# Routing each token to its two chosen experts: sorted row tiles through DRAM instead of eight dense experts

## The chip, the cores and the metric

The kernel runs on one core of one Trainium2 chip. The metric is the device time of one launch in microseconds (us). TensorE (PE) does the matrix products and writes them to PSUM; VectorE (DVE), ScalarE (ACT) and GpSimd (POOL) are the other compute engines; SyncE (SP) only issues transfers here. Each engine takes its own instructions in the order of the compiled program, and an instruction that waits holds up all that stand behind it on its engine. All data is 32-bit floating point.

## What is computed

One layer works on x of shape (8, 1024, 256): 8 sequences, 1024 time steps, 256 features. Four sublayers follow one another, each on a layer norm of x and added to x: a gated linear attention with its own feed-forward part, a mixture of experts, a small recurrence over time, and the same mixture of experts again.

```python
x = x + attn_a(layernorm(x))      # gated scan over time per head, output projection, GELU FFN
x = x + ffn(layernorm(x))         # mixture of experts "a" in the kernel
x = x + attn_b(layernorm(x))      # h = tanh(x_t B + h A^T), state of 16; y = h C W_out^T + b
x = x + ffn(layernorm(x))         # mixture of experts "b"

def ffn(x):                       # 8 experts, each a 256x256 matrix, 2 per token
    probs = softmax(x @ router_w.T)
    topk_vals, topk_idx = top_k(probs, 2)
    topk_w = topk_vals / (topk_vals.sum(-1) + 1e-6)
    # sum over the two chosen: (x @ W[expert] + its probability) * its weight
```

## The kernel before

The 1024 time steps are cut into 16 groups of 64. A group holds 64 steps of all 8 sequences: 512 tokens, which are 4 tiles (`j`) of 128 tokens by 256 features. The main loop is a software pipeline over 19 steps. Step s does the attention of group s, experts "a" of group s-1, the recurrence of group s-2 and experts "b" of group s-3. The text of the kernel is not the order of execution: the framework's scheduler merges the streams when it compiles, so that each engine has a fixed queue in which the work of four groups is interleaved.

- `layernorm` takes statistics on DVE, one reciprocal square root on POOL (L296, tile `rstd_*`) and the scaling on DVE (L298). So every layer norm passes through POOL's queue.
- `transposed` (L313) turns 128x128 blocks on PE and copies them out on ACT.
- `attention`: projections (L333); the values go through DRAM (`vd`, L475) and come back replicated as four tiles `S` of 1 MB (L481), loaded on SP's queue into four buffers. DVE multiplies (L516), scans over time (16 scans, L524) and multiplies again (L530); PE adds up the state per head (`po`, L535). Then come a norm, the output projection, a second layer norm (`h2`), and the feed-forward part (L578, L342). `others` (called between these pieces) places pieces of the experts' work.
- `moe` routes on the 512 tokens (L379 to L409, some thirty small DVE operations and one ACT exponential). It then multiplies **all** tokens with **all** experts: for each tile `j` four PSUM tiles of two experts each (L418, 512 columns), and DVE adds each expert's part, scaled by a weight that is zero for six of the eight (L427). The bias of a tile is added on POOL (L412).
- `recurrence` is a strict chain of 64 steps per group: a 16x16 matrix product on PE (L613), then a tanh on ACT (L621).

An f32 matrix product is two records in the profile (L418 has 1024 instructions and 2048 records, 1024 in each of its two groups); a transpose is one.

Of the kernel before, what the change touches and what calls it, by code (L numbers as in the profile page):

```python
# [9 lines left out]
F32 = mybir.dt.float32  # L10
AF = mybir.ActivationFunctionType
ALU = mybir.AluOpType
AX = mybir.AxisListType
PSUM = bass.MemoryType.PSUM

P = 128
EPS = 1e-5
# [3 lines left out]
def kernel(  # L21
# [27 lines left out]
    nc = tc.nc  # L49
    NB, T, D = x.shape  # L50
# [6 lines left out]
    NE = router_w.shape[0]  # L57
# [15 lines left out]
    loads = ctx.enter_context(tc.tile_pool(name="loads", bufs=2))  # L73
    ps_mm = ctx.enter_context(tc.tile_pool(name="ps_mm", bufs=2, space=PSUM))
    ps_mx = ctx.enter_context(tc.tile_pool(name="ps_mx", bufs=1, space=PSUM))
    ps_e = ctx.enter_context(tc.tile_pool(name="ps_e", bufs=2, space=PSUM))
# [5 lines left out]
    def mm_tile(name, part="a"):  # L82
        pool = ps_mm if part == "a" else ps_mx
        return pool.tile([P, 512], F32, tag=f"mm_{part}", name=name)

# [21 lines left out]
    rev = const.tile([P, NT, NE], F32, name="rev")  # L107
    for e in range(NE):
        nc.vector.memset(rev[:, :, e : e + 1], float(NE - e))

# [169 lines left out]
    states = ctx.enter_context(tc.tile_pool(name="states", bufs=4))  # L280
    dram = ctx.enter_context(tc.tile_pool(name="dram", bufs=2, space=bass.MemoryType.DRAM))
    small = ctx.enter_context(tc.tile_pool(name="small", bufs=3))
# [68 lines left out]
    def moe(xs, name):  # L351


        yT = transposed(layernorm(xs, name, "m"), name, "m")
        pl = mm_tile(f"pl_{name}", "m")
        for j in range(NT):
            for c in range(KC):
                nc.tensor.matmul(
                    pl[:, j * NE : (j + 1) * NE],
                    yT[:, c, j * P : (j + 1) * P],  # L360
                    rw_t[:, c, :],
                    start=(c == 0),
                    stop=(c == KC - 1),
                )
        logits = pl[:, : NT * NE].rearrange("p (j e) -> p j e", e=NE)

        def row(nm):
            return small.tile([P, NT], F32, tag=f"m_{nm}", name=f"{nm}_{name}")

        def mat(nm):  # L370
            return small.tile([P, NT, NE], F32, tag=f"m_{nm}", name=f"{nm}_{name}")

        def wide(r):
            return r.unsqueeze(2).to_broadcast([P, NT, NE])

        mx, den, m1, m2 = row("mx"), row("den"), row("m1"), row("m2")
        probs, left, sc, one, two = mat("probs"), mat("left"), mat("sc"), mat("one"), mat("two")
        top = row("top")
        nc.vector.tensor_reduce(mx, logits, AX.X, ALU.max)  # L379
        nc.vector.tensor_tensor(probs, logits, wide(mx), ALU.subtract)  # L380
        nc.scalar.activation(probs, probs, AF.Exp)
        nc.vector.tensor_reduce(den, probs, AX.X, ALU.add)
        nc.vector.reciprocal(den, den)
        nc.vector.tensor_tensor(probs, probs, wide(den), ALU.mult)

        nc.vector.tensor_reduce(m1, probs, AX.X, ALU.max)
        nc.vector.tensor_tensor(sc, probs, wide(m1), ALU.is_equal)
        nc.vector.tensor_tensor(sc, sc, rev, ALU.mult)
        nc.vector.tensor_reduce(top, sc, AX.X, ALU.max)
        nc.vector.tensor_tensor(one, sc, wide(top), ALU.is_equal)  # L390
        nc.vector.scalar_tensor_tensor(left, one, -2.0, probs, ALU.mult, ALU.add)
        nc.vector.tensor_reduce(m2, left, AX.X, ALU.max)
        nc.vector.tensor_tensor(sc, left, wide(m2), ALU.is_equal)
        nc.vector.tensor_tensor(sc, sc, rev, ALU.mult)
        nc.vector.tensor_reduce(top, sc, AX.X, ALU.max)
        nc.vector.tensor_tensor(two, sc, wide(top), ALU.is_equal)

        w1r, w2r, rs, bias = row("w1r"), row("w2r"), row("rs"), row("bias")
        nc.vector.tensor_tensor(rs, m1, m2, ALU.add)
        nc.vector.tensor_scalar_add(rs, rs, 1e-6)  # L400
        nc.vector.reciprocal(rs, rs)
        nc.vector.tensor_tensor(w1r, m1, rs, ALU.mult)
        nc.vector.tensor_tensor(w2r, m2, rs, ALU.mult)
        nc.vector.tensor_tensor(one, one, wide(w1r), ALU.mult)
        nc.vector.tensor_tensor(two, two, wide(w2r), ALU.mult)
        nc.vector.tensor_tensor(one, one, two, ALU.add)
        nc.vector.tensor_tensor(w1r, w1r, m1, ALU.mult)
        nc.vector.tensor_tensor(w2r, w2r, m2, ALU.mult)
        nc.vector.tensor_tensor(bias, w1r, w2r, ALU.add)  # L409

        def experts(j):
            nc.gpsimd.tensor_scalar(  # L412
                xs[:, j, :], xs[:, j, :], 1.0, bias[:, j : j + 1], ALU.mult, ALU.add
            )
            for ep in range(NE // 2):
                pe = ps_e.tile([P, 2, D], F32, tag="e", name=f"pe_{name}_{j}_{ep}")
                for c in range(KC):
                    nc.tensor.matmul(  # L418
                        pe,
                        yT[:, c, j * P : (j + 1) * P],  # L420
                        we_t[:, c, 2 * ep : 2 * ep + 2, :],
                        start=(c == 0),
                        stop=(c == KC - 1),
                    )
                for k in range(2):
                    e = 2 * ep + k
                    nc.vector.scalar_tensor_tensor(  # L427
                        xs[:, j, :],
                        pe[:, k, :],
                        one[:, j, e : e + 1],  # L430
                        xs[:, j, :],
                        ALU.mult,
                        ALU.add,
                    )

        return [partial(experts, j) for j in range(NT)]
# [3 lines left out]
    def attention(g, xg, between):  # L440


        between = list(between)

        def others(n):
            for work_of_others in between[:n]:
                work_of_others()
            del between[:n]
# [8 lines left out]
        z = work.tile([P, COLS], F32, tag="z", name=f"z_{g}", bufs=1)  # L457
        nc.scalar.activation(z, pz, AF.Identity, bias=gb2_t)
        az = work.tile([P, COLS], F32, tag="az", name=f"az_{g}", bufs=1)
# [8 lines left out]
        kT = work.tile([P, COLS], F32, tag="kT", name=f"kT_{g}")  # L468
        vT = work.tile([P, KC, COLS], F32, tag="vT", name=f"vT_{g}", bufs=1)
# [76 lines left out]
        oT = work.tile([P, KC, COLS], F32, tag="oT", name=f"oT_{g}", bufs=1)  # L546
        sq = work.tile([P, KC, COLS], F32, tag="sq", name=f"sq_{g}", bufs=1)
# [9 lines left out]
        others(2)  # L557
        for c in range(KC):
            nc.vector.tensor_tensor(oT[:, c, :], po[c], rs, ALU.mult)
        nc.vector.tensor_mul(oT, oT, sgT)  # L560

        xa = work.tile([P, NT, D], F32, tag="xa", name=f"xa_{g}")
# [5 lines left out]
        x1 = work.tile([P, NT, D], F32, tag="x1", name=f"x1_{g}", bufs=4)  # L568
        nc.gpsimd.tensor_add(x1, xg, b2_t.unsqueeze(1).to_broadcast([P, NT, D]))
        nc.gpsimd.tensor_add(x1, x1, xa)  # L570
# [15 lines left out]
        for jp in range(NT // 2):  # L586
            pr = by_token(fT, w2_t, FC, jp, f"pw2_{g}_{jp}")
            js = slice(2 * jp, 2 * jp + 2)
            nc.vector.tensor_add(x1[:, js, :], pr, x1[:, js, :])  # L589
        return x1  # L590
# [32 lines left out]
    def recurrence_out(g, x2):  # L623
        hs = hs_t[g % NHS]
        x3 = work.tile([P, NT, D], F32, tag="x3", name=f"x3_{g}")
        for jp in range(NT // 2):
            py = mm_tile(f"py_{g}_{jp}", "m")
            for jj in range(2):
# [10 lines left out]
                x3[:, js, :], py.rearrange("p (j m) -> p j m", j=2), x2[:, js, :]  # L639
            )  # L640
        return x3
# [3 lines left out]
    x1s, x3s, u_s = {}, {}, {}  # L645
    for step in range(NG + 3):
        ga, gm, gr, gz = step, step - 1, step - 2, step - 3
        between = []
        if 0 <= gr < NG:
            recurrence(gr, u_s.pop(gr))  # L650
        if 0 <= gz < NG:
            x3s[gz] = recurrence_out(gz, x1s.pop(gz))
            between += moe(x3s[gz], f"b{gz}")
        if 0 <= gm < NG:
            between += moe(x1s[gm], f"a{gm}")
        if ga < NG:
            xg = x_next
            if ga + 1 < NG:
                x_next = load_x(ga + 1)
            x1s[ga] = attention(ga, xg, between)  # L660
        else:
            for work_of_others in between:
                work_of_others()
        if 0 <= gz < NG:
            x3 = x3s.pop(gz)
            for b in range(BT):
                nc.sync.dma_start(
                    out=out_v[b, gz * TG : (gz + 1) * TG, :, :],
                    in_=x3[b * TG : (b + 1) * TG, :, :],
                )  # L670
        if 0 <= gm < NG:
            u_s[gm] = recurrence_in(gm, x1s[gm])
# [53 lines left out]
```

## Time and profile before

| what | value |
|---|---|
| median of 3 runs | 2548.77 us (2548.24 to 2550.33) |
| the profiled execution's own time | 2542.61 us |
| its span in the profile | 2540.8 us |
| granted PE clock, mean | 0.88 |
| busy share PE, DVE, ACT, POOL | 86%, 63%, 25%, 12% |
| indirect transfers | none |
| transfers issued by POOL | 2, both at the start |

A line of the profile's groups names the source line, engine, operation, and the tiles (output, then inputs), the shapes, the count, the busy time in all, and the mean of one. What stands behind the second bar is the time that the engine idled just before these instructions, and what ended that idle time. A line of the timeline gives the start, the duration, and the same names. The busy time of PE is no measure of its peak, since matrix products overlap with one another; the distance from one start to the next in a dense row of them is.

### The profile page before, as it was taken

Reading aid. Unit: us, or ns where it says so; the run is one execution under the profiler, and the core shown is the slowest. Engines: PE = TensorE matmul, PEld = TensorE weight load, DVE = VectorE, ACT = ScalarE, POOL = GpSimd, SP = SyncE. Lnnn points to the kernel's source line nnn. Section 1 sums busy time; section 2 is a strip of 40 time slices with the busy share of each in tenths; the row PEclk is TensorE's granted clock in tenths of the full one; section 3 lists DMA queues with packets and bytes.
Section 4 is the critical chain, followed back from the end, with each engine's and each line's share of the span. In section 5 each row is a group of like instructions: output and inputs, shape, how many; then the busy total and the mean of one; then the engine's idle time right before and its main releaser. Section 6 shows DMA issues by size and latency. Waiting matters only on the chain.

```text
span 2540.8 us, 22420 instructions
## 1 busy us (share of the span) xinstructions
PE 2183.9 (86%) x7505; PEld 966.4 (38%) x7505; DVE 1600.2 (63%) x3877; ACT 631.4 (25%) x1657; POOL 305.7 (12%) x264
## 2 busy tenths in 40 slices
PE   3478898988989898898989889898998989988987
PEld 1234342433434243343434334243343434334333
DVE  4675858567574857757475674856747576573534
ACT  2123242141413213131321313214131221312010
POOL 1101010121111111101111201112011111110000
PEclk9598988989999898988979798897988979798978
DMA  5130303030302103030020302103030030300000
GB/s 155 26 75 9 75 9 75 17 75 17 75 9 50 35 16 75 17 75 9 26 58 17 75 9 61 27 13 75 17 75 9 1 75 9 75 9 1 9 0 17
DMA packets 37893, 98.39 MB, mean 39 GB/s; under 512 B 4666, under 2 KB 25203, under 8 KB 29587
## 3 DMA queue, kind: packets, MB, share of 16 engines
q1 hardware_dynamic: 33664, 94.64, 15.7%
q10 hardware_dynamic: 4034, 2.17, 0.3%
q8 instruction: 61, 1.00, 0.2%
q14 instruction: 54, 0.43, 0.1%
q0 software_dynamic: 80, 0.14, 0.0%
HBM read 80.17 MB, written 16.78 MB: 38 GB/s over the span
## 4 chain that ended last, share of the span: by engine, by line
PE 62%; DVE 21%; ACT 7%; issue 5%; POOL 2%; DMA 2%; ACTq 0%; POOLq 0%; SPq 0%; DVEq 0%
PE pe_b L418 18%; PE pe_a L418 9%; DVE x L427 6%; PE pu L613 5%; DVE S L524 5%; PE pw L342 4%; PE po L535 3%; ACT hs L621 3%; PE pf L578 3%; PE pu L597 2%; PE pg L333 2%; PE py L630 2%; PE pz L333 2%; PE pt_h L313 2%; DVE S L516 2%
## 5 line engine op out<-in xcount | busy, mean ns | idle before, releaser
L418 PE MATMUL pe_b<-we,yT_b 128*128 128x512 f32 x1024 | 570.2, 674 | 32.8 <-DVE x L427 27.7
L418 PE MATMUL pe_a<-we,yT_a 128*128 128x512 f32 x1024 | 466.7, 604 | 23.6 <-DVE x L427 14.2
L427 DVE SCALAR_TENSOR_TENSOR x<-pe_b,one_b,x 128x256 f32<-128x256 f32 x512 | 240.5, 476 | 225.3 <-PE pe_b L418 220.8
L613 PEld LDWEIGHTS pu<-hs,at 16*16 16x16 f32 x2046 | 115.5, 94 | 599.3 <-ACT hs L621 348.8
L613 PE MATMUL pu<-hs,at 16*16 16x8 f32 x2046 | 216.9, 176 | 140.0 <-ACT hs L621 139.7
L621 ACT ACTIVATE hs<-pu 16x8 f32<-16x8 f32 x1024 | 176.0, 172 | 637.6 <-PE pu L613 634.2
L524 DVE TENSOR_TENSOR_SCAN S<-decay,S 128x512 f32<-128x512 f32 x256 | 306.2, 1210 | 0.0
L427 DVE SCALAR_TENSOR_TENSOR x<-pe_a,one_a,x 128x256 f32<-128x256 f32 x512 | 244.4, 478 | 97.5 <-PE pe_a L418 87.6
L418 PEld LDWEIGHTS pe_a<-we,yT_a 128*128 128x128 f32 x1024 | 191.1, 192 | 265.2 <-issue 232.2
L418 PEld LDWEIGHTS pe_b<-we,yT_b 128*128 128x128 f32 x1024 | 185.9, 205 | 251.2 <-issue 194.7
L516 DVE TENSOR_TENSOR S<-S,kT 128x2048 f32<-128x2048 f32 x64 | 145.6, 2275 | 16.4 <-DMA S<-vd 16.4
L535 PE MATMUL po<-S,head_pad 128*32 128x512 f32 x512 | 122.1, 828 | 39.2 <-DVE S L530 38.6
L530 DVE TENSOR_TENSOR S<-S,qT 128x2048 f32<-128x2048 f32 x64 | 146.1, 2283 | 0.0
L412 POOL TENSOR_SCALAR x<-x,bias_a 128x256 f32<-128x256 f32 x64 | 102.0, 1608 | 295.4 <-DVE bias_a L409 295.4
L570 POOL TENSOR_TENSOR x<-x,xa 128x1024 f32<-128x1024 f32 x16 | 37.6, 2347 | 815.5 <-DVE mv_h L292 803.8
L321 ACT ACTIVATE yT_h<-pt_h,lnb,lnw 128x512 f32<-128x512 f32 x64 | 47.9, 776 | 323.6 <-PE pt_h L313 323.5
L578 PE MATMUL pf<-yT_h,w 128*128 128x512 f32 x256 | 121.4, 621 | 1.7 <-ACT yT_h L321 1.7
L589 DVE TENSOR_TENSOR x<-pw,x 128x512 f32<-128x512 f32 x32 | 22.1, 691 | 147.1 <-PE pw L342 147.1
L549 ACT ACTIVATE sq<-po 128x512 f32<-128x512 f32 x32 | 19.1, 597 | 380.8 <-PE po L535 380.8
L342 PE MATMUL pw<-w,fT 128*128 128x256 f32 x512 | 113.1, 379 | 0.0
L342 PEld LDWEIGHTS pw<-w,fT 128*128 128x128 f32 x512 | 97.3, 190 | 20.1 <-issue 7.7
L638 DVE TENSOR_TENSOR x<-py,x 128x512 f32<-128x512 f32 x32 | 22.1, 690 | 123.2 <-PE py L630 123.2
(193 smaller groups left out, 2318.1 us busy)
## 6 DMA issues: line engine op xcount, KB each, us to landing
S<-vd SPq DMA_DIRECT2D x64, 1024.0 KB, 12.8
x<-in_L_attn_a_x_dram SPq DMA_DIRECT2D x32, 256.0 KB, 3.9
vd<-vT SPq DMA_DIRECT2D x16, 512.0 KB, 2.8
out_dram<-x SPq DMA_DIRECT2D x32, 256.0 KB, 3.2
we<-_ffn_expert_weights_dram SPq DMA_DIRECT2D x8, 256.0 KB, 4.7
w<-in_L_attn_a_W_dram ACTq DMA_DIRECT2D x2, 512.0 KB, 6.3
wo<-in_L_attn_a_Wo_dram SPq DMA_DIRECT2D x16, 16.0 KB, 2.3
wv_raw<-in_L_attn_a_Wv_dram ACTq DMA_DIRECT2D x1, 256.0 KB, 3.8
```

What stands on the lines that cost most here:

```text
L333: nc.tensor.matmul(ps, w[:, c, :], rhsT[:, c, :], start=(c == 0), stop=(c == KC - 1))
L342: nc.tensor.matmul(ps[:, jj * D : (jj + 1) * D], lhsT[:, c, j * P : (j + 1) * P], w[:, c, :], start=(c == 0), stop=(c == n_k - 1),)
L412: nc.gpsimd.tensor_scalar(xs[:, j, :], xs[:, j, :], 1.0, bias[:, j : j + 1], ALU.mult, ALU.add)
L418: nc.tensor.matmul(pe, yT[:, c, j * P : (j + 1) * P], we_t[:, c, 2 * ep : 2 * ep + 2, :], start=(c == 0), stop=(c == KC - 1),)
L427: nc.vector.scalar_tensor_tensor(xs[:, j, :], pe[:, k, :], one[:, j, e : e + 1], xs[:, j, :], ALU.mult, ALU.add,)
L516: nc.vector.tensor_tensor(S_f, S_f, kT.unsqueeze(1).to_broadcast([P, VQ, COLS]), ALU.mult)
L524: nc.vector.tensor_tensor_scan(S_f[:, j, :], decay_f, S_f[:, j, :], 0.0, ALU.mult, ALU.add)
L530: nc.vector.tensor_tensor(S_f, S_f, qT.unsqueeze(1).to_broadcast([P, VQ, COLS]), ALU.mult)
L535: nc.tensor.matmul(po[c][32 * j : 32 * j + 32, :], head_pad[:, NH * (1 - i) : NH * (1 - i) + 32], S_f[:, j, :], start=(i == 0), stop=(i == 1),
L578: nc.tensor.matmul(pf, w1_t[:, c, f * P : (f + 1) * P], h2T[:, c, :], start=(c == 0), stop=(c == KC - 1),)
L613: nc.tensor.matmul(pu[:, t, :], at_t, before, start=False, stop=True, skip_group_check=True,)
L621: nc.scalar.activation(hs[:N, :, t], pu[:, t, :], AF.Tanh)
```

## The change

The experts' part is computed for the two chosen experts only.

- Each token is copied twice into a DRAM buffer, at places that are sorted by expert. Routing computes the places: counts per tile by two small matrix products (`pn`, new lines 467 and 468), running sums, and each expert's rows rounded up to whole tiles of 128. A register list `eidi` says which expert owns each row tile.
- The copy is an indirect DMA on POOL's queue: two for each tile of 128 tokens (new L535), 128 rows of 1 KB each.
- A piece `expert(ip)` loads two row tiles from DRAM on SP's queue (L548), reads the two expert numbers into PE registers (L549), transposes (L560), copies on ACT (L564), multiplies by the register-chosen expert (L568, 256 columns), copies on ACT (L576) and stores to a second DRAM buffer (L577).
- `combine` fetches each token's two results with two indirect DMAs per tile (L584, tile `got`, two buffers) and adds them, scaled, on DVE (L590).
- A call now spans a block of two groups; nine blocks of 1, 2, 2, 2, 2, 2, 2, 2 and 1 groups take 12 steps in place of 19. A block of two groups has 2048 chosen rows and 24 row tiles (12 pieces); a block of one has 1024 rows and 16 row tiles (8 pieces).
- The tile bias moves from POOL to ACT (L542). To make room in SBUF, x is updated in place and has nine buffers, the `S` tiles have three buffers, and some tiles share space. The keys and queries are projected ahead of the values.

```diff
+BLOCKS = [1] + [2] * 7 + [1]
...
-    states = ctx.enter_context(tc.tile_pool(name="states", bufs=4))
+    states = ctx.enter_context(tc.tile_pool(name="states", bufs=3))
+    rows = ctx.enter_context(tc.tile_pool(name="rows", bufs=2))
...
-        def experts(j):
-            nc.gpsimd.tensor_scalar(
-                xs[:, j, :], xs[:, j, :], 1.0, bias[:, j : j + 1], ALU.mult, ALU.add
-            )
-            for ep in range(NE // 2):
-                pe = ps_e.tile([P, 2, D], F32, tag="e", name=f"pe_{name}_{j}_{ep}")
+        rows_in, rows_out = (t[: NTL * P, :] for t in rows_dram[name[0]])
+        for j in range(NJ):
+            for s in range(2):
+                nc.gpsimd.indirect_dma_start(
+                    out=rows_in,
+                    out_offset=bass.IndirectOffsetOnAxis(ap=posi[:, s, j : j + 1], axis=0),
+                    in_=ys[j // NT][:, j % NT, :],
+                    in_offset=None,
+                )
+            x_j = xs[j // NT][:, j % NT, :]
+            nc.scalar.activation(x_j, x_j, AF.Identity, bias=bias[:, j : j + 1])
...
+        def expert(ip):
+            r = rows.tile([P, 2, D], F32, tag="r", name=f"r_{name}_{ip}")
+            nc.sync.dma_start(out=r, in_=in_v[:, 2 * ip : 2 * ip + 2, :])
+            _, ids = nc.values_load_multi_w_load_instructions(
+                eidi[0:1, 2 * ip : 2 * ip + 2],
+                engines=[mybir.EngineType.PE],
...
+            for k in range(2):
                 for c in range(KC):
                     nc.tensor.matmul(
-                        pe,
-                        yT[:, c, j * P : (j + 1) * P],
-                        we_t[:, c, 2 * ep : 2 * ep + 2, :],
+                        pe[:, k, :],
+                        rT[:, k, c, :],
+                        we_t[:, c, bass.ds(ids[k], 1), :],
                         start=(c == 0),
                         stop=(c == KC - 1),
                     )
...
+            nc.sync.dma_start(out=out_v_[:, 2 * ip : 2 * ip + 2, :], in_=ro)
+
+        def combine():
+            for j in range(NJ):
+                x_j = xs[j // NT][:, j % NT, :]
+                for s, w in enumerate((w1r, w2r)):
+                    e = rows.tile([P, D], F32, tag="got", name=f"got_{name}_{j}_{s}")
+                    nc.gpsimd.indirect_dma_start(
+                        out=e,
+                        out_offset=None,
+                        in_=rows_out,
+                        in_offset=bass.IndirectOffsetOnAxis(ap=posi[:, s, j : j + 1], axis=0),
+                    )
                     nc.vector.scalar_tensor_tensor(
-                        xs[:, j, :],
...
+                        x_j, e, w[:, j : j + 1], x_j, ALU.mult, ALU.add
                     )
...
+    for step in range(NK + 3):
+        ba, bm, br, bz = block(step), block(step - 1), block(step - 2), block(step - 3)
...
+        for i, g in enumerate(ba):
+            n = -(-len(between) // (len(ba) - i))
+            mine, between = between[:n], between[n:]
...
+            attention(g, xg, mine)
+            x1s[g] = xg
+        for work_of_others in between + last:
+            work_of_others()
```

## The prediction

> **What bounds the kernel now.** I read the page's engine shares first, then the chain that ended last.
>
> ```profile
> span 2540.8 us, 22420 instructions
> ...
> PE 2183.9 (86%) x7505; PEld 966.4 (38%) x7505; DVE 1600.2 (63%) x3877; ACT 631.4 (25%) x1657; POOL 305.7 (12%) x264
> ...
> PE 62%; DVE 21%; ACT 7%; issue 5%; POOL 2%; DMA 2%; ACTq 0%; POOLq 0%; SPq 0%; DVEq 0%
> ```
>
> PE holds 62% of the chain, DMA 2%, POOL 2%: PE sets the pace, and no transfer is on the path. The groups by line show the experts, and POOL's bias op beside each kind of DVE work:
>
> ```profile
> L418 PE MATMUL pe_b<-we,yT_b 128*128 128x512 f32 x1024 | 570.2, 674 | 32.8 <-DVE x L427 27.7 <-DVE S_last L527 2.5 <-DVE one_a L390 0.7
> L418 PE MATMUL pe_a<-we,yT_a 128*128 128x512 f32 x1024 | 466.7, 604 | 23.6 <-DVE x L427 14.2 <-DVE S_last L527 5.6 <-issue 3.5
> L427 DVE SCALAR_TENSOR_TENSOR x<-pe_a,one_a,x 128x256 f32<-128x256 f32 x512 | 244.4, 478 | 97.5 <-PE pe_a L418 87.6 <-POOL x L412 2.4
> L412 POOL TENSOR_SCALAR x<-x,bias_a 128x256 f32<-128x256 f32 x64 | 102.0, 1608 | 295.4 <-DVE bias_a L409 295.4
> L412 POOL TENSOR_SCALAR x<-x,bias_b 128x256 f32<-128x256 f32 x64 | 29.6, 479 | 250.9 <-DVE bias_b L409 250.9
> ```
>
> The mean of one overlaps its neighbours, so I price PE from dense rows of the timeline (start, duration, count last):
>
> ```profile
> 2287.67 9.61 PE L418 MATMUL pe_a<-we,yT_a 128*128 128x512 f32 x22
> 2305.43 7.07 PE L342 MATMUL pw<-w,fT 128*128 128x256 f32 x32
> 2312.34 0.60 PE L313 MATMUL pt_yr<-ident,y_yr 128*128 128x128 f32 x4
> ```
>
> One 512-column record takes 9.61/22 = 0.437 us, a 256-column one 0.221, a transpose 0.15.
>
> **The compute that goes and comes.** Out: 2048 records x 0.437 = 895 us of PE; 1024 DVE additions, 485 us (244.4 + 240.5); 132 us of POOL (L412). In: 18 calls have 2x(2x8 + 7x12) = 200 pieces. Each piece is 4 transposes (0.60) and 8 records of 256 columns (1.77): 2.37 us, 474 us in all. Rounding to whole tiles is in that: 24 row tiles stand against 64 dense ones, not 16. Each piece also makes PE read registers, 200 reads, which the trace does not show. Bounds: 0, and 1.28 us (an ACT table load, the trace's one row of an engine fetching before it goes on). I take the middle, 0.64: 128 us. The skill's page "DMA: Bandwidth & Descriptors" (Latency and other measured facts) gives such a load a floor of some 600 ns; by it the term would be 120. PE is left with 895 - 474 - 128 = 293 us less. DVE gains 256 additions x 0.48 = 123 and loses 485; routing adds some 22 small operations of 0.2 us per call, but 18 calls replace 32, about nothing. ACT gains 400 copies x 0.58 (L317's mean) and 128 bias operations at 0.4 (below the 0.58 of a copy twice as wide), 283 us: 36% busy, in cover.
>
> Small edits, at nothing: SP issues 400 transfers more (two take 1.30 us: 260 us), under waits for POOL. With three `S` buffers the fourth load waits until the first tile is used up; it is needed some 28 us after the first, and a load takes 12.8 (issue rows): without that cover, up to 12.8 per group. Keys and queries ahead of the values put `vd` off by 8 records, 3.5 us per group, where an attention is exposed.
>
> If PE still set the end: 2541 - 293 = 2248.
>
> **The 512 indirect transfers.** They are what the trace of before cannot show. The compiled order settles their form. All 512 stand in POOL's one queue. Each of a block's 16 scatters waits for the semaphore of the scatter before it, as all write one DRAM tensor. The gathers go two at a time, since `got` has two buffers, each freed by its addition on DVE. And POOL's queue also holds the `rstd` of every layer norm: what stands behind a waiting scatter is the attention's next norm, then DVE and PE behind that. The nearest rows are issues (KB each, us to landing last) and POOL's own time to issue one:
>
> ```profile
> 1.28 0.74 POOL L131 DMA_DIRECT2D b<-in_L_attn_a_b_dram  x1 [0.35 <-issue]
> ```
> ```profile
> x<-in_L_attn_a_x_dram SPq DMA_DIRECT2D x32, 256.0 KB, 3.9
> vd<-vT SPq DMA_DIRECT2D x16, 512.0 KB, 2.8
> out_dram<-x SPq DMA_DIRECT2D x32, 256.0 KB, 3.2
> b<-in_L_attn_a_b_dram POOLq DMA_DIRECT2D x1, 128.0 KB, 5.3
> ```
>
> - A scatter: 2.8 at least (`vd`, issue included), 0.74 + 5.3 = 6.04 at most (POOL's own transfer, in the crowded start). I take the store out of mid-run plus POOL's issue, 0.74 + 3.2 = 3.94: same direction, same stage.
> - A gather, half of a round of issue, landing and addition: (0.74 + 2.8 + 0.48)/2 = 2.01 to (0.74 + 5.3 + 0.48)/2 = 3.26; I take (0.74 + 3.9 + 0.48)/2 = 2.56.
>
> Scatter and gather together, s = 6.50, between 4.8 and 9.3. There are 256 of each.
>
> The rows are of larger transfers (256 KB for 128), which speaks for less. L412 speaks for more: beside the attention's scans the same POOL operation takes 1608 ns for 479. Some 60% of the 88 scatters of experts "b" in steps 3 to 8 lie beside scans (37.6 of 63 us); were the issue stretched as L412 is, 0.74 to 2.5, that is 53 x 1.76 = 93 us. I let the two cancel and keep the 93 for the upper end. The skill's page "SBUF — State Buffer" (A bandwidth-pool intuition that's wrong (but worth ruling out)) speaks against the change too: GpSimd is locked out of writing its descriptors while DVE holds the shared port, 620 ns becoming 3100. No transfer here shows it; by that figure 53 scatters would cost 131 us more.
>
> **Where they stand on the path.** In a full step the compiled order of POOL and DVE is a ring: layer norms and routing of "b"; 16 scatters of b; the second norm of the step's first attention; 16 scatters of a; 16 gathers of b; the second norm of the second attention; 16 gathers of a; then the next step's norms. b's pieces run under a's scatters (63 us against 12 x 4.5 = 54), a's under b's gathers and the second attention; the recurrence (128 x 0.47, a dense step of L613 and L621, is 60 us) under b's scatters. So a full step is 16 pairs twice, 32 s, plus what POOL waits for:
>
> ```profile
> 952.30 1.02 POOL L296 TENSOR_TENSOR rstd_b<-ve_b,neghalf 128x4 f32<-128x4 f32 x1 [0.17 <-DVE mv_a L292]
> ...
> 969.96 1.85 POOL L412 TENSOR_SCALAR x<-x,bias_b 128x256 f32<-128x256 f32 x4 [13.99 <-DVE bias_b L409]
> ```
> ```profile
> 29.67 1.02 POOL L296 TENSOR_TENSOR rstd_h<-ve_h,neghalf 128x4 f32<-128x4 f32 x1 [3.06 <-DVE ve_h L294]
> ...
> 112.82 1.02 POOL L296 TENSOR_TENSOR rstd_h<-ve_h,neghalf 128x4 f32<-128x4 f32 x1
> ```
>
> From a norm to routed takes 17.7 us for one group; with two groups and more operations I take 27. The norms between take about 8 after b's scatters and 15 before a's gathers (908.66 to 922.67 in the timeline). Together 50. Where DVE's order puts the second attention's scans behind the gathers of b, their 38 us (16 x 1.21 + 8 x 2.28) and the 18 to the next norm are exposed: 56 in steps 3 and 5, 30 in step 4 (scans partly earlier), none in 6 and 7. The sum, from step 3 on:
>
> - Steps 0 to 2: one attention alone takes 83 us (the two rows above). Its second norm at 113, feed-forward 20 and routing 27 make 160; then 8 scatters, 32 of pieces, 8 gathers, the scans behind them 56, feed-forward and routing 55, 16 scatters, the next attention's projections and scans 72, 16 gathers and routing 27: 402 + 24 s.
> - Steps 3 to 7: 24 s + 106, 32 s + 80, 32 s + 106, 32 s + 50, 32 s + 50; step 8: 32 s + 50; step 9: 24 s + 35.
> - Steps 10 and 11, with nothing to run b's pieces under: 16 s + 75 and 8 s + 55.
>
> That is 1009 + 256 s. With s = 6.50: 1009 + 1664 = 2673 us of span. The profiled execution lies 1.8 above its span, the median 6.2 above that, so 2673 + 8 = 2681; I say 2680.
>
> So the end moves from PE to POOL's queue: PE's 293 us come off, and are not on the path any more. A full step takes 258 to 314 us, against 304 for two groups before (`rstd_b` goes from 345.0 to 2323.66 in 13 steps, 152 each). The loss stands at the end, where the pipeline empties in steps of two groups: steps 8 to 11 sum to 735; before, the same stretch, from the fifteenth group's attention on, took some 2541 - (345 + 12 x 152) = 372.
>
> **Rivals.**
> - *Short transfers, faster.* Quiet 128 KB transfers come in near the `vd` row. The ring equals the time of before at s = (2541 - 1009)/256 = 5.98, and decides for faster below it. At s = 4.8 it gives 2238, where PE (2248) takes over: about 2256 with the 8. For it: the rows I took are of twice the bytes. Against: an indirect transfer must also read its indices, which no row prices.
> - *Long transfers, far slower.* Descriptors held up by DVE or made row by row: s above 8 gives over 3065, at 9.3 with the 93 above 3491. For it: the 1608 against 479.
> - *The recurrence sets the pace.* Two groups in one step are 128 links. At 0.47 us they are 60 us; with one 512-column product between (1.19, from 2458.59 to 2459.78 in the timeline) 152. Both lie inside a step of 258, so it changes nothing; the time stays 2680.
>
> **How the numbers follow.** The forecast, s from 5.98 to 8, gives 2553 to 3065 and has 0.45; short transfers 0.36; long ones 0.16; that the two effects meet within 0.2% (5 us, about what a measurement can tell from no change) 0.03. Slower is 0.45 + 0.16 = 0.61. The range goes down to the PE bound, 2250, and up to 3250, s = 8.7, which leaves out about a tenth at each end.
>
> **What would show it.** Right: POOL's queue waiting for its own transfers (`rows_a_in`, `rows_b_in`, `got`) on top of the chain, PE below 65% busy, first scatters to last some 63 us per 16, a step of two groups at 258 to 314 us, some 735 us from step 8 on. Wrong: PE still over 80% busy with L568 and L560 on the chain; consecutive scatters under 3 us apart, or over 6; or PE waiting long at the register read L549.

## The result: 363 us slower, and the profile after

| | before | after |
|---|---|---|
| median of the runs | 2549.55 us (4 runs) | 2912.27 us (4 runs) |
| ratio after to before, 95% interval | | 1.141 [1.137, 1.145] |
| span of the profiled execution | 2540.8 us | 2909.4 us |
| mean granted TensorE clock | 0.881 | 0.749 |

The forecast was 2680 us, in a range of 2250 to 3250. The sign was right and the time lies inside the range, but 363 us were lost where 131 were expected. First the page's engine shares and its costliest groups for the kernel after (columns as before):

```profile
span 2909.4 us, 25546 instructions
...
PE 1925.9 (66%) x8057; PEld 1113.3 (38%) x8057; DVE 1306.0 (45%) x3081; ACT 887.6 (31%) x2182; POOL 739.2 (25%) x649
...
L568 PE MATMUL pe_a<-we,rT_a 128*128 x800 | 233.7, 438 | 55.7 <-ACT rT_a L564 54.8
L535 POOL DMA_INDIRECT rows_a_in<-y_a,posi_a x128 | 150.4, 1175 | 440.1 <-DMA rows_a_in<-y_a,posi_a 274.5
L535 POOL DMA_INDIRECT rows_b_in<-y_b,posi_b x128 | 149.7, 1169 | 432.2 <-DMA rows_b_in<-y_b,posi_b 217.9
L568 PE MATMUL pe_b<-we,rT_b 128*128 x800 | 218.6, 418 | 44.5 <-ACT rT_b L564 43.0
L584 POOL DMA_INDIRECT got_b<-rows_b_out,posi_b x128 | 132.5, 1035 | 312.0 <-DVE x L590 144.0
L584 POOL DMA_INDIRECT got_a<-rows_a_out,posi_a x128 | 126.1, 985 | 251.3 <-DVE x L590 104.2
```

PE is down from 86% to 66% of the span, as the forecast wanted. The scatters (L535) and gathers (L584) are on POOL, with 1436 us of idle time before them. Only 492 of those are scatters waiting for the scatter before (274.5 + 217.9). The other large waits are for routing (363 us for `posi_a` and `posi_b`), for the additions on DVE that free `got` (248) and for expert outputs (183). (The chain of waits breaks off on this page after the last few instructions, all at 0%, so I read POOL's queue in its place.) The timeline of POOL in step 6, the first that the prediction took at 32 s + 50; the last bracket is the idle time before the row and what ended it:

```profile
1572.06 0.94 POOL L584 DMA_INDIRECT got_a<-rows_a_out,posi_a  x1 [0.77 <-DVE x L590]
...
1631.39 2.94 POOL L535 DMA_INDIRECT rows_b_in<-y_b,posi_b  x1 [39.40 <-DVE posi_b L507]
1636.06 1.60 POOL L535 DMA_INDIRECT rows_b_in<-y_b,posi_b  x1 [1.72 <-DMA rows_b_in<-y_b,posi_b]
...
1642.68 0.96 POOL L535 DMA_INDIRECT rows_b_in<-y_b,posi_b  x1 [1.70 <-DMA rows_b_in<-y_b,posi_b]
1645.34 0.96 POOL L535 DMA_INDIRECT rows_b_in<-y_b,posi_b  x1 [1.71 <-DMA rows_b_in<-y_b,posi_b]
...
1711.86 0.96 POOL L535 DMA_INDIRECT rows_a_in<-y_a,posi_a  x1 [20.57 <-DVE posi_a L507]
```

One scatter takes 0.96 us to issue and 1.70 until it has landed: 2.66 from one to the next (1642.68 to 1645.34). At the start of the series, where DVE's scans and products on `S` run at the same time, the issue is stretched to 1.6 to 2.9 us. The two large brackets are waits for routing, of b and of a. With the same reading of the whole step, from the last gather of one step to the last of the next:

| POOL in that step, 1573 to 1886 us | measured | forecast |
|---|---|---|
| norms and routing of b | 58 | 27 |
| 16 scatters of b, with one norm among them | 60 | 63 |
| routing of a | 21 | 0 |
| 16 scatters of a | 63 | 63 |
| gathers of b (with 5 of waiting for stores) and of a | 50 + 31 | 41 + 41 |
| norms between them | 29 | 8 + 15 |
| sum | 313 | 258 |

Why routing takes 58 and not 27 is in DVE's timeline, and why a's starts so late too:

```profile
1597.85 0.22 DVE L452 TENSOR_TENSOR sc_b<-sc_b,rev 128x64 f32<-128x64 f32 x1
1597.99 1.22 DVE L689 TENSOR_TENSOR_SCAN S<-decay,S 128x512 f32<-128x512 f32 x1
1599.13 0.19 DVE L453 TENSOR_REDUCE top_b<-sc_b 128x8 f32<-128x64 f32 x1
1599.24 1.21 DVE L689 TENSOR_TENSOR_SCAN S<-decay,S 128x512 f32<-128x512 f32 x1
...
1692.84 1.38 DVE L345 TENSOR_SCALAR y_a<-x,mv_a,rstd_a 128x256 f32<-128x256 f32 x4 [6.78 <-DMA rows_b_in<-y_b,posi_b]
...
1711.41 0.17 DVE L507 CAST posi_a<-pos_a 128x16 uint32<-128x16 f32 x1
```

Between two routing operations of 0.2 us the compiled order puts a scan of 1.2. And a's normed rows (`y_a`) wait for b's last scatter: the tag `y_m` has two buffers, both hold b's rows until they are scattered.

Step by step (ends read at the last gather of a, in POOL's timeline): steps 0 to 2 end at 591 us (forecast 558), steps 3 to 7 take 318, 324, 340, 313 and 307 (forecast 262, 288, 314, 258, 258), step 8 takes 285 (258), steps 9 to 11 431 (477). At the end of step 7 the kernel is 24 us behind the kernel before at the same attention (2193 against 345 + 12 x 152 = 2169), and what follows takes 716 us against 372. Those are not the same work: with blocks of two, experts "b" have then been done for 9 groups, where the kernel before has done them for 12. `dense2` below tells the two apart.

### The profile page after: what moved, and what is told of

It is laid out like the page before. It is cut to its first block, busy times and chain, and to the rows that moved or that the text cites. A ratio compares the mean times of both kernels' runs of the same rounds, so it can differ in the third digit from the quotient of the medians.

```text
span 2909.4 us, 25546 instructions
## 1 busy us (share of the span) xinstructions
PE 1925.9 (66%) x8057; PEld 1113.3 (38%) x8057; DVE 1306.0 (45%) x3081; ACT 887.6 (31%) x2182; POOL 739.2 (25%) x649
## 5 line engine op out<-in xcount | busy, mean ns | idle before, releaser
L568 PE MATMUL pe_a<-we,rT_a 128*128 x800 | 233.7, 438 | 55.7 <-ACT rT_a L564 54.8
L535 POOL DMA_INDIRECT rows_a_in<-y_a,posi_a x128 | 150.4, 1175 | 440.1 <-DMA rows_a_in<-y_a,posi_a 274.5
L535 POOL DMA_INDIRECT rows_b_in<-y_b,posi_b x128 | 149.7, 1169 | 432.2 <-DMA rows_b_in<-y_b,posi_b 217.9
L568 PE MATMUL pe_b<-we,rT_b 128*128 x800 | 218.6, 418 | 44.5 <-ACT rT_b L564 43.0
L568 PEld LDWEIGHTS pe_a<-we,rT_a 128*128 128x128 f32 x800 | 164.0, 216 | 127.6 <-ACT rT_a L564 84.2
L584 POOL DMA_INDIRECT got_b<-rows_b_out,posi_b x128 | 132.5, 1035 | 312.0 <-DVE x L590 144.0
L681 DVE TENSOR_TENSOR S<-S,kT 128x2048 f32<-128x2048 f32 x64 | 145.9, 2279 | 122.1 <-DMA S<-vd 106.9
L568 PEld LDWEIGHTS pe_b<-we,rT_b 128*128 128x128 f32 x800 | 154.3, 204 | 106.9 <-ACT rT_b L564 83.1
L584 POOL DMA_INDIRECT got_a<-rows_a_out,posi_a x128 | 126.1, 985 | 251.3 <-DVE x L590 104.2
L560 PE MATMUL prt_a<-ident,r_a 128*128 128x128 f32 x400 | 70.5, 304 | 165.7 <-DMA r_a<-rows_a_in 165.7
L590 DVE SCALAR_TENSOR_TENSOR x<-got_b,w1r_b,x 128x256 f32<-128x256 f32 x64 | 35.1, 548 | 295.1 <-DMA got_b<-rows_b_out,posi_b 295.0
L576 ACT COPY ro_a<-pe_a 128x512 f32<-128x512 f32 x100 | 58.5, 585 | 297.3 <-PE pe_a L568 208.2
L560 PE MATMUL prt_b<-ident,r_b 128*128 128x128 f32 x400 | 65.8, 290 | 100.3 <-DMA r_b<-rows_b_in 100.3
L560 PEld LDWEIGHTS prt_a<-ident,r_a 128*128 128x128 f32 x400 | 54.8, 157 | 195.0 <-issue 157.5
```

The source lines that it names most:

```text
L535: nc.gpsimd.indirect_dma_start(out=rows_in, out_offset=bass.IndirectOffsetOnAxis(ap=posi[:, s, j : j + 1], axis=0), in_=ys[j // NT][:, j % ...
L560: nc.tensor.transpose(pt[:, n * P : (n + 1) * P], r[:, k, c * P : (c + 1) * P], ident)
L568: nc.tensor.matmul(pe[:, k, :], rT[:, k, c, :], we_t[:, c, bass.ds(ids[k], 1), :], start=(c == 0), stop=(c == KC - 1),)
L576: nc.scalar.copy(ro, pe)
L584: nc.gpsimd.indirect_dma_start(out=e, out_offset=None, in_=rows_out, in_offset=bass.IndirectOffsetOnAxis(ap=posi[:, s, j : j + 1], axis=0),)
L681: nc.vector.tensor_tensor(S_f, S_f, kT.unsqueeze(1).to_broadcast([P, VQ, COLS]), ALU.mult)
```

## The experiments

All are single runs of one kernel unless an interval is given; the kernel before took 2547 to 2571 us beside them. The four runs of the changed kernel lie between 2904 and 2917, so differences of some 13 us say nothing. Gains are counted from 2912.

**What the transfers cost.** Three kernels leave them out; in `no_gather` the addition reads `ys[j // NT][:, j % NT, :]`.

```
-            for s in range(2):
-                nc.gpsimd.indirect_dma_start(out=rows_in, ...)        # no_scatter, no_indirect
-                    e = rows.tile([P, D], F32, tag="got", ...)
-                    nc.gpsimd.indirect_dma_start(out=e, ...)
+                    e = ys[j // NT][:, j % NT, :]                      # no_gather, no_indirect
```

`no_scatter`: 

> The 256 scatters are left out (the sorted rows stay zero); routing, loads, products, gathers and additions stay. In the changed kernel's profile the scatters hold POOL for 792 us (150 + 150 busy, 274 + 218 waiting for their own transfer). Theory A, the transfers in POOL's queue lie on the path: the 425 us of the a scatters come off at least, so 2250 to 2500 us. Theory B, the path runs through the waits between the engines (norms, routing and two attentions a step in a fixed order), and transfers fill time that would be spent waiting anyway: under 200 us come off, over 2700.

Measured 2622.79.

`no_gather`: 

> The 256 gathers are left out; the additions that combine read the normed rows in SBUF in their place. The gathers hold POOL for 639 us (133 + 126 busy, the rest waiting for the additions, without the 183 that wait for expert outputs). Theory A: 400 to 640 us come off, 2270 to 2500. Theory B: the waits for expert outputs and for the second attention stay, over 2700.

Measured 2683.61.

`no_indirect`: 

> Scatters and gathers both left out; all products, loads and stores of rows stay, and the additions read the normed rows. Theory A: nothing but PE is left to set the pace, 2300 to 2400 us, PE over 80% busy. Theory B: 2600 us or more, PE under 75% busy and POOL waiting for DVE's norms as before.

Measured 2372.56. So the scatters are worth 290 us, the gathers 229, both together 540, little more than the sum of 519. But these are 540 of the 1051 us (792 for scatters alone, 259 for the gathers' issue) that they hold POOL at the least. For either alone neither theory had it (A forecast 410 to 660 off for the scatters, B under 200); with both out A's 2300 to 2400 holds, with PE at 79% for its "over 80%". These kernels also cut what hung on the transfers: without scatters nothing holds the two buffers of `y` for them, and without gathers the additions no longer wait for expert outputs. So the 540 us are the transfers together with their couplings, not the transfers alone.

`open_scatter` keeps all work and takes the wait away, as the rows of a block differ:

```
+                tc.declare_no_dep(sc_i.ins, group=f"sc_{name}", reason=...)
+                tc.add_to_no_dep_group(f"sc_{name}", sc_i.ins)
```

> All work kept; the scatters of one block, which write different rows, no longer wait for one another (each waits only for the one eight before it). A scatter should hold POOL for its issue, about 1.0 + 0.3 us, in place of 3.1. Theory A: 256 x 1.8 = 460 us less on POOL, of which the half that lies beside the first attention's scans may stay hidden: 2450 to 2690 us. Theory B: 2800 to 2900.

Measured 2802.24, a gain of 110. The timeline of POOL in its step from 1493 to 1815 us:

```profile
1558.57 2.94 POOL L535 DMA_INDIRECT rows_b_in<-y_b,posi_b  x1 [46.75 <-DVE posi_b L507]
...
1566.24 0.96 POOL L535 DMA_INDIRECT rows_b_in<-y_b,posi_b  x1 [0.30 <-issue]
1567.51 0.96 POOL L535 DMA_INDIRECT rows_b_in<-y_b,posi_b  x1 [0.30 <-issue]
...
1613.59 0.96 POOL L535 DMA_INDIRECT rows_a_in<-y_a,posi_a  x1 [28.70 <-DVE posi_a L507]
...
1670.99 1.03 POOL L588 DMA_INDIRECT got_b<-rows_b_out,posi_b  x1 [27.73 <-DMA rows_b_out<-ro_b]
```

The edit did what it should: 1.27 us from scatter to scatter (1566.24 to 1567.51), 16 in 26 us for b and 20 for a, where they took 60 and 63. And the step still takes 322 us: the 77 us came back as longer waits for b's routing (46.8 us, 39.4 in step 6 above), for a's (28.7 for 20.6), for the expert outputs (27.7 for 5.4) and, behind the lines shown, for a norm of the second attention (59.2 for 15.3). Theory A falls here as a law for the step; theory B's 2800 to 2900 holds, at its lower edge.

**What else could it be: the blocks, the recurrence.** `dense2` keeps the blocks of two and the new attention and computes all eight experts (the old `experts` loop over a block's tiles, no rows in DRAM).

> Blocks of two groups and the changed kernel's attention, but all eight experts computed for every token as before: no scatter, no gather, no register reads. If the blocks cost only the longer emptying at the end, some 150 us, and the keys and queries that are projected twice 56 us of PE: 2700 to 2760. If the blocks cost nothing: 2550 to 2610. If most of the 363 us lost comes from the blocks: over 2800.

Measured 2579.79, in the range for blocks that cost nothing: 30 us, with the doubled projections in it. Where they lie shows in the copy that ends each quarter of an attention's scans (before, `dense2`, after; the number before the semicolon is the start of the last one):

```profile
L527 DVE COPY S_last<-S x64: 170/183/380, 65.0 to 2252.5; 128x32 f32<-128x32 f32 x64
L581 DVE COPY S_last<-S x64: 166/186/287, 64.1 to 2120.8; 128x32 f32<-128x32 f32 x64
L692 DVE COPY S_last<-S x64: 163/186/195, 78.5 to 2269.4; 128x32 f32<-128x32 f32 x64
```

From there to the end of the span it is 288 us before, 457 in `dense2` and 640 after. So 169 of the 352 us by which the emptying is longer come with the blocks of two, which leave more work over; `dense2` had gained 132 us ahead of this point for it. Against `dense2` the sparse kernel loses 149 us up to the last scans and 183 behind them. `blocks1` is the reverse, `BLOCKS = [1] * 16`:

> The changed kernel with blocks of one group (16 blocks; 8 pieces per call in place of 12 per two groups, 256 pieces of 2.37 us in place of 200). Theory A: the same 512 transfers, a shorter emptying at the end: 2750 to 2900. Theory B: the waits of a step (norms, routing, expert outputs) come once per group instead of once per two: 3000 or more.

Measured 3086.66: the steps' waits come per step, as theory B had it (the 28% more pieces are in it too).

`no_recur` replaces the linked loop by one `tanh` per group, and `before_no_recur` does the same to the kernel before:

> The recurrence's chain is left out: one tanh per group in place of 64 linked pairs of a product and a tanh. Theory of the prediction: the links lie beside other work, 2880 to 2912. Rival: the 1024 links, 0.47 us each when nothing stands between (481 us in all), hold PE's and ACT's queues, in order, ahead of routing and experts: 2500 to 2750.

Measured 2734.57, 178 less. That looked like a cause.

> A control for no_recur: the kernel before, with the recurrence's chain left out in the same way. If the 178 us that no_recur gained on the changed kernel are a cost of the new order, this gains clearly less, under 100 us (2450 or more). If the links cost both kernels the same, it gains 150 to 220 us, as PE was busy with them for 217 us: 2330 to 2400; then they are no part of what the change lost.

Measured 2337.58, 209 less. The links cost the kernel before even more: they are no part of the loss.

**Order and buffers, one at a time.** Each is the changed kernel with one edit.

```
scans_after: +  with tc.issue_after(<the cast to posi of b and of a>): <the first attention's scans>
a_first:     the call and the additions of a are written ahead of those of b
adds_after:  +  with tc.issue_after(<last scan product of the step>): <combine of b and of a>
four_y:      y_m bufs=4 in place of 2; kT, qT bufs=1 in place of 2
```

`scans_after`: 

> The first attention's scans are queued on DVE behind the routing of both calls of the step (order alone; no work is changed). In the changed kernel's steps of two groups POOL waits 39 to 49 us for posi_b and 17 to 22 for posi_a, because scans of 1.2 and 2.3 us stand between routing operations of 0.2. Theory B (waits between engines set the pace): 20 to 30 us less in each of the five full steps and some in the others, 2750 to 2820 us. Theory A (the transfers set the pace; a wait saved before them returns behind them, as the scans then run later): within 30 us of 2912.

Measured 2883.13, 29 less: just inside A's range. Theory A's reason, that the scans then run later and what waits for them does too, was not traced further.

`a_first`: 

> In each step the call for a is put ahead of the call for b, and its additions too (order alone). What b computes goes to the output only; what a computes is what the recurrence and the next step's b need. Theory B (the order in the queues makes the waits): a's scatters no longer wait 60 us behind b's, 2750 to 2850 us. Theory A (the transfers set the pace, whatever their order): within 30 us of 2912.

Measured 2800.02, 112 less, with not a transfer changed: theory B.

`adds_after`: 

> The additions of gathered rows are queued on DVE behind the scans of the step's last attention (order alone). In the changed kernel DVE waits 407 us for gathered rows of b, and POOL 53 to 84 us a step in steps 3 and 5 for the second attention's norm behind them. Theory B: 80 to 150 us less, 2760 to 2830. Theory A: within 30 us of 2912.

Measured 2860.51, 52 less: between the two ranges.

`four_y`: 

> The normed rows y have four buffers in place of two (keys and queries one each, to make room); nothing else. With two, the call for a can't write its normed rows before b's scatters have read theirs, so a's routing starts behind b's last scatter: POOL waits 17 to 22 us for posi_a in each full step, 59 in step 3, 154 in all. If that coupling is on the path: 2760 to 2850 us. If it only moves the wait elsewhere: 2880 to 2912.

Measured 2797.98, 114 less. With `a_first`'s 112 it is the largest of the four; the two can't be told apart, and both bear on a's wait behind b. In its timeline b's and a's scatters alternate in one series, and the wait for `posi_a` falls from 20.6 to 3.4 us.

**All transfers cheaper, then in another order.** `open_deep` is `open_scatter` with `got` at `bufs=6` and the second projection of keys and queries kept alone; `all_orders` adds `a_first` and `adds_after`.

`open_deep`: 

> All work kept: scatters of a block not waiting for one another, six buffers for gathered rows in place of two, keys and queries projected once. Each transfer should hold POOL for some 1.3 us in place of 3.1 and 2.5, 700 us less over 512. Theory A: 2400 to 2600 us. Theory B: what POOL saves comes back as waits for norms, routing and expert outputs, as it did with open scatters alone (2802): 2720 to 2800.

Measured 2777.46: theory B. The deep gathers and the spared projections are worth 25 us on top of the open scatters.

`all_orders`: 

> open_deep with a ahead of b and the additions behind the last attention's scans. If both the transfers' time and the order of the queues make the loss, each hides behind the other and only both together free the step: 2400 to 2550 us. If the recurrence's links in PE's queue hold the rest: 2600 or more.

Measured 2739.84, in the range of "2600 or more", but the links need not be why. In its waits two faults of this order show: a's additions had been pinned behind the scans with b's (POOL waited 337.5 us in `got_a` for them), and `posi_b` came 54 to 57 us after a's scatters, since `y` still had two buffers.

`uncoupled` mends both: `four_y`, `scans_after`, `a_first` and `open_deep` together, only b's additions behind the last scans, and one buffer for the attention's own normed rows.

> All work kept: open scatters, six buffers for gathered rows, keys and queries once, four buffers for y (one for the attention's), a ahead of b, both routings ahead of the first attention's scans, b's additions behind the last attention's scans. If the couplings through buffers and queue order are what puts 540 us of transfers on the path, a full step falls to the 267 to 280 us that it has without indirect transfers, against 302 to 313: 2450 to 2580 us. If a step stays at 300 or more, something not yet named holds it: 2700 or more.

Measured 2544.28: all 512 transfers are there, and the kernel is 368 us faster than the changed one, as much as the change had cost. `open_deep` (2777) has the same open scatters, gather buffers and projections, so the order and the buffers of `y`, keys and queries alone are worth 233 us here. They were not run together with the slower transfers, so how much of the 233 needs the cheap ones is open. The windows of two of its full steps and of its emptying (start and end, length, then busy time and instructions of PE, PEld, DVE, ACT, POOL, granted clock, DMA share, GB/s):

```profile
1153.50:1439.90 286.40, 233.24 (x978) 131.03 (x977) 160.04 (x366) 104.49 (x267) 97.04 (x81) 0.82 0.40 114
1439.90:1726.90 287.00, 233.32 (x978) 131.43 (x976) 160.11 (x366) 104.42 (x267) 95.34 (x80) 0.82 0.40 114
2007.10:2542.60 535.50, 359.95 (x1774) 225.53 (x1773) 156.66 (x484) 156.86 (x510) 178.52 (x171) 0.75 0.39 118
```

A full step takes 287 us with all transfers, and PE is busy for 233 of them. Without indirect transfers (`no_indirect`) it took 267 to 280. So nearly all of the transfers' time can hide in a full step. What remains is the emptying, 535 us with PE two thirds busy; behind the last scans it is 472 us, against 457 in `dense2`.

**The emptying.** `uncoupled_tail` ends in three blocks of one, `BLOCKS = [1] + [2] * 6 + [1] * 3`:

> The same with the last two blocks of two and one replaced by three blocks of one group, so that the pipeline empties in steps of one group. From the last attention on, all_orders took some 545 us against 372 before the change. If the emptying is a chain of one block's transfers and products per step, it shrinks: 40 to 100 us less than uncoupled. If the waits of a step cost the same for one group as for two (as blocks1 showed, 3087): the same or slower.

Measured 2547.09: the same. The emptying did shrink, from 472 to 357 us behind the last scans, but these came 118 us later (2188 for 2070). `short_tail` is `uncoupled` with the order changed after the last attention (products behind the links; b's gathers and additions behind the next block's scatters and routing):

> uncoupled, with the emptying put in order: after the last attention a block's products stand on PE behind the recurrence's links, and b's gathers and additions behind the next block's routing and scatters (a second tensor for expert outputs of b). In uncoupled the last 535 us go to a chain in which b's three blocks follow one another and the links, 0.47 us when dense, take over a us each between products (128 in 170 us). If that chain sets the end: 60 to 130 us less, 2410 to 2485. If transfers and loads of one block after another set it: 2530 to 2545.

Measured 2556.97 (10 runs), ratio to the kernel before 0.999 [0.995, 1.003]: the same, so this order does not shorten the emptying. It put the products so far back that b's next norm waited 48 us for them; whether a better order exists was not tried, and the links are not ruled out by it.

`dense_tail` is `uncoupled` with the last four calls dense, `dense=not ba`, and the old loop over experts in `moe`:

> uncoupled, but in the three steps after the last attention (one call of a for one group, three of b for five groups) all eight experts are computed, without transfers. There, PE is 21 to 60% busy in uncoupled and a call is a chain of routing 25 to 30, scatters 20, loads and products 50 to 70, gathers 20 us; dense it is routing and 28 us of products per group. If the emptying is that chain: the last 535 us shrink by 80 to 160, 2380 to 2465. If the recurrence's links set it: less than 40 off, 2505 or more.

Measured 2481.51 us (4 runs), ratio to the kernel before 0.971 [0.964, 0.979]: faster than both kernels, though the gain of 63 stays under the 80 to 160 expected. Its windows:

```profile
2007.00:2200.00 193.00, 168.43 (x794) 96.31 (x794) 90.34 (x207) 70.56 (x223) 81.47 (x68) 0.82 0.47 138
2200.00:2484.00 284.00, 267.59 (x852) 109.61 (x852) 125.33 (x357) 43.32 (x201) 4.03 (x4) 0.88 0.04 10
```

In the last 284 us PE is busy for 268: the chain of transfers is gone, and PE, busy for 94% of it, sets the end there. That is the likely reason why the gain stops short.

## Why the prediction was right on the sign and wrong on the size

**PE's term.** Forecast 293 us less (895 - 474 - 128). From the kernel before to `no_indirect` PE's busy time goes from 2183.9 to 1868.1, 316 less: near, but in part by luck, as two errors pull in opposite directions. The register reads were taken at 128 us, between 0 and 256. They are in the trace of the kernel after:

```profile
L549 PEldq TENSOR_LOAD <-eidi_a x100: 532/538/1412, 206.8 to 2634.2; - x100
L549 PEldq TENSOR_LOAD <-eidi_b x100: 532/874/1305, 713.4 to 2879.8; - x100
```

One takes 0.53 to 1.41 us, 154 us in all, so 0.64 was a fair size. But in 195 of the 200 a product starts while the read runs, and PE is idle for less than 2 us of the 154: what was wrong was to add them to PE's time. And I read the diff's two added lines for keys and queries as a move; the old two lines are still there, so both products are made twice (`pk` and `pq` count 128 records each for 64): 128 x 0.437 = 56 us of PE that the sum left out. (`dense2` makes them twice too; from it to `no_indirect`, which differ in the whole of the experts' part, PE's busy time falls by 386 us, from 2254.3, and the time by 207.)

**The transfers' prices.** Right in size, a little high. A scatter holds POOL for (150.4 + 149.7 + 274.5 + 217.9)/256 = 3.10 us against 3.94, a gather 639/256 = 2.5 against 2.56 (in step 6 above 2.0 for a and 2.8 for b); in that step 32 pairs' worth is some 200 us against 208. The stretch beside DVE, kept at 93 us for the upper end, is (150.4 + 149.7) - 256 x 0.96 = 54 us. By the figures of the Trainium skill's page "SBUF — State Buffer" (A bandwidth-pool intuition that's wrong (but worth ruling out)) the estimate was 131. The runs show the effect, at a lower price: the 52 scatters whose issue overlaps DVE's scans and products on `S` take 1.91 us in the mean, the 204 others 0.98.

**The step that failed: what POOL waits for between the transfers.** I summed 50 us per full step; it was 113 in step 6 (58 + 21 + 29, and 5 of waiting for stores). "From a norm to routed takes 17.7 us for one group; with two groups and more operations I take 27" held in step 5, where routing stood ahead of the scans (31), and not in steps 6 and 7 (58 and 74), where it stands among them; the compiled order showed it, and I used it only for the second attention. And a's routing was taken as done by the time b's scatters end; with two buffers for `y` it can't begin before. `four_y` prices that at 114 us. Over the steps the sum was too low by 282 us in steps 0 to 8 and too high by 46 in steps 9 to 11.

**The formula itself.** "A full step is 32 s + 50" makes each microsecond of a pair cost 256 in all. Measured, `open_scatter` took 443 us off the time that scatters hold POOL (with the gaps between issues, 809 to 366 us) and gained 110; leaving scatters out (792 us) gave 290. POOL's queue is one of several chains that wait for one another: shorten one, and the routing, the stores or the next norm is late next. So the rival "short transfers, faster" failed as well, though its condition was nearly met: s was 5.6 in the mean and 6.2 in step 6, for which the sum gives some 2440 to 2600 us. That also says that the sign was in part luck. With the measured mean the same sum is faster than before; a price taken too high stood in for waits taken too short. What was missing was the couplings: with them removed and the transfers made cheaper (`uncoupled`) the time is 2544, with the transfers made cheaper alone (`open_deep`) 2777.

**Where the loss stands.** "Steps 8 to 11 sum to 735" was nearly met (716), but by two errors: step 8 took 285 us for 258, steps 9 to 11 431 for 477. And the forecast had steps 0 to 7 end at 1938 us, 231 ahead of the kernel before; they ended at 2193, 24 behind. Its reason for the long end, the emptying in steps of two groups, is half of it: behind the last scans `dense2` takes 169 us longer than the kernel before, though it had gained 132 ahead of them. The other 183 us come with the sparse calls. A sparse call is a chain of routing, scatters, loads and products, and gathers, with little to run beside it once the attentions are done; `dense_tail` shows 63 us of it, the rest is not priced.

**The other rival.** The recurrence is not the cause, as said, but "both lie inside a step, so it changes nothing" is wrong: without it the kernel takes 178 us less, and the kernel before 209.

**The small edits, put at nothing.** DVE waits 107 us in all for the tiles `S` to be loaded (L681), where it waited 16 before (L516) and 41 in `dense2`. Three buffers, and SP's queue with the pieces' transfers in it, are the likely reasons. `uncoupled` waits 109 us and is 368 us faster, so this does not separate the two; whether it lies on the path of either was not tested.

**What would show it.** Of the signs of being right: PE at 66% (under 65 said), a step of two groups at 285 to 340 us (258 to 314 said), 16 scatters in 60 to 63 us in step 6 (63 said). One sign of being wrong was there too, "consecutive scatters under 3 us apart": in a dense series they are 2.66 apart, and the mean is higher only where issues or landings are stretched.

## What to carry to other kernels

Moving work from a busy engine to a chain of transfers pays only for what the queue orders and buffers let run beside it; count, for each buffer, who must be done before the next writer may start, not only how long each transfer takes. A price per transfer times their number was an upper bound here (792 us of scatters, 290 gained without them): test it by making the transfer cheap and see whether the step gets shorter. In this kernel the sparse form paid where there was other work to cover its latency, and the dense one where the pipeline empties; where it fills, this was not tried.

## What the runs showed of the hardware

- An indirect DMA of 128 rows of 1 KB takes POOL 0.96 us to issue and lands 2.4 to 2.9 us after (medians of the four kinds). POOL issues one per 2.66 us when each waits for the one before, and one per 1.27 us when it does not (`open_scatter`).
- The mean granted TensorE clock was lower in kernels with PE less busy: 0.90 at 87% (`dense2`), 0.82 at 79% (`no_indirect`), 0.80 at 73% (`uncoupled`), 0.75 at 66% (after). The share alone does not fix it: without the recurrence's links it was 0.905 at 80% (`before_no_recur`) and 0.764 at 60% (`no_recur`). In the kernel after, the same eight records of a piece took 3.68 us behind a wait (granted clock 0.54 in that stretch) and 1.99 us in a dense stretch (1.00):

```profile
1718.08 3.68 PE L568 MATMUL pe_b<-we,rT_b 128*128 x8 [2.18 <-ACT rT_b L564]
...
1722.92 1.99 PE L568 MATMUL pe_b<-we,rT_b 128*128 x8
```

  So a price from a dense row is too low for a piece that starts behind a wait. Whether the idle time lowers the clock was not tested, and what share of the 363 us lies in the clock was not priced.
- A register read by PE (L549) lasts 0.53 to 1.41 us, but 195 of the 200 ran while products went on, and they left PE idle for less than 2 us in all (19 us in `uncoupled`).
